# Four fused layers with windowed attention: the last half chunk of keys multiplied with V for both batches at once

## The chip, the cores and the metric

The kernel is one launch on one core of a Trainium2 chip. The metric is device time in microseconds (us), the median of several executions. A separate execution was recorded by the hardware profiler; its rows are called the trace here, and their sums the page. Engines are PE (TensorE matmuls; PEld is its loading of weights), DVE (VectorE), ACT (ScalarE), POOL (GpSimd) and SP (SyncE, which here only issues DMAs). L123 is line 123 of the kernel before.

## The reference

There are 64 batches of 64 tokens with 512 features, all in float32, and four layers, each added to its input:

```python
x = x + (einsum('bsi,bio->bso', x, W0[id]) + b0[id][:, None, :])     # a weight per batch
x = x + x @ W.T + delta                                              # LoRA: adapter per batch, rank 16
x = x + attention(x)                                                 # below
x = x + (einsum('bct,bcd->bdt', x, w3[subjects]) + bias[:, :, None]) # over the tokens of a batch
```

The attention has 8 query heads and 4 heads of keys and values, 64 wide. Queries and keys get an RMS norm and a rotary turn by their position `pos = kv_lens + t`. New keys and values are written into a cache of blocks; a query sees the positions from `pos - 255` to `pos`:

```python
allowed = (kpos <= pos) & (kpos > pos - WINDOW)       # WINDOW = 256
p = softmax(where(allowed, q @ k_all.T * SCALE, -inf))
o = (p @ v_all) @ Wo.T
```

So the 64 queries of a batch see a window of at most 319 positions, held as 320: two chunks of 128 and a half chunk of 64.

## The kernel before

The work goes by 32 tiles of 128 tokens, two batches each. Instructions run on each engine in the order in which the program issues them; that order is written out by hand, and the engines wait for each other by semaphores that follow from the tiles of memory they share. `bank()` hands out one bank of PSUM after the other from a ring of seven; an eighth (`pyp`) is for py.

**Phase 1 (lines 185 to 753, about 0 to 541 us).** For each tile: layer 0 with the two batches' gathered weights (`layer0`, L249: 128 rows by 64 columns, one batch in each half of the array; `add_bias`, L260, adds the bias to x on POOL), transposes (`turn0`, L273), layer 1 (L620 to L643), transposes back (L654), keys and values (L140, pk), and for older tiles the query product (pq), its norm and rotary turn (`turned`, L116 to L135) and transposes (`turn_q`, L170), whose result `qTs` goes by DMA to `qTd` in memory. Keys and values of each tile are stored to `kvd` (keep_kv). Old rows of the cache are fetched in the background by `copies` (a gather into `st` on POOL, L155, and a store to `kvd` on SP, L161 and L164): `other(i)` (L704) lets one or two of them go with each tile i > 5, and the last ones are stored when phase 1 ends. The biases come transposed through PE (`pb`) ahead of layer 0 of tile 0 (L668 to L673).

**Between the phases (L956 to L974).** SP issues the loads for phase 2: keys and values, queries, masks of tiles 0 and 1, `wo`, the query of tile 2. The queries of the last eight tiles (`LATE`) are made only here: product, `parts_q` on DVE and ACT, `turn_q`. Their `qTs` has two buffers in the pool `late`. `keys(0)` transposes the first tile's keys. The query of the last tile, 31, is made inside steps 0 to 3 of phase 2.

**Phase 2 (L975 to L1008, about 541 to 953 us).** Step s of the loop runs, in program order:

- `scores(s)`: eight products ps (L841), one bank each; DVE takes each with its mask and its maximum (L849, `pr` and `mx`), ACT the exponential (L853).
- `attend(s-1)`: the weights times V (L888), described below, and the copy of the sum `po` to `oT` (L906).
- `normalise(s)` on DVE (L861, L865): divides by the sums.
- on even s from 4 on `last(s-4)`: layer 3 of two tiles (pz, L928); then `project(s-2)`: times Wo (py, L916), added to x (L920).
- `keys(s+1)`: transposes of the next keys (pkt, L822, L828), copied by ACT (L823, L829).
- at s = 3 and 4 `turn_q` of a late query.
- `turn(s)`: transposes of the weights `pr` (ppt). For each of the four groups of heads g one bank with four blocks of 128 by 128 (L874: two full chunks of each of the two batches), copied to `pT[:, g]` by DVE and ACT in turn (L875). A fifth bank (L878) has the half chunks: `pr[:, g, 256:384]` is the half chunk of batch 0 next to that of batch 1, so that after the transpose partitions 0 to 63 hold batch 0's 64 positions and 64 to 127 batch 1's, each for the queries of both heads. ACT copies it whole to `pT[:, 4]` (L879).

`attend` sums in two banks, one per batch (`po[b2]`). 16 products have 128 positions each (tiles of 128 rows by 64 columns: two groups of heads share the array's columns). Eight more are for the half chunk, each with the 64 partitions of its batch (64 rows by 64 columns, a quadrant of the array). Each product is two instructions on PE.

Of the kernel before, what the change touches and what calls it, by code (L numbers as in the profile page):

```python
# [12 lines left out]
F32 = mybir.dt.float32  # L13
# [7 lines left out]
B, T, D = 64, 64, 512  # L21
NTOK = B * T
KC = D // 128
E = 16
NA, RANK = 8, 16
H, G, HD = 8, 4, 64
# [24 lines left out]
NT = NTOK // 128  # L51
# [8 lines left out]
def body(ctx: ExitStack, tc: tile.TileContext, a: dict, out: bass.AP):  # L60
    nc = tc.nc
    V, S, P, TE = nc.vector, nc.scalar, nc.gpsimd, nc.tensor
# [27 lines left out]
    late = ctx.enter_context(tc.tile_pool(name="late", bufs=1))  # L90
# [8 lines left out]
    def bank(name):  # L99
        return ring.tile([128, 512], F32, tag="ring", name=name)  # L100
# [65 lines left out]
    def run(parts):  # L166
        for _ in parts:
            pass

    def turn_q(i):  # L170
        qrf = qrs.pop(i)
        pqt = bank("pqt")
        for c in range(KC):
            TE.transpose(pqt[:, c * 128 : (c + 1) * 128], qrf[:, c * 128 : (c + 1) * 128], ident)  # L174
        qT = late.tile([128, 2, 2, 2, T], F32, name="qTs", bufs=2)
        for gp in range(2):
            S.copy(
                qT[:, gp].rearrange("p b h t -> p h b t"),
                pqt[:, gp * 256 : (gp + 1) * 256].rearrange("p (h b t) -> p h b t", h=2, b=2),
            )  # L180
        nc.sync.dma_start(
            qTd[i * 128 : (i + 1) * 128, :], qT.rearrange("p g b h t -> p (g b h t)")
        )

    with ExitStack() as pa:
# [57 lines left out]
        def layer0(i, bias=True):  # L243

            p0 = bank("p0")
            for c in range(KC):
                for h in range(2):
                    hs = slice(h * T, (h + 1) * T)
                    TE.matmul(p0[hs, :], xs[i][:, c, hs], w0s[i][h][:, c, :], start=c == 0, stop=c == KC - 1)  # L249
            w0s.pop(i)  # L250
            s0 = s0s[i] = wk.tile([128, D], F32, name="s0")
            S.copy(s0, p0)
            if bias:
                add_bias(i)

        def add_bias(i):

            x1 = x1s[i] = x1p.tile([128, KC, 128], F32, name="x1")
            for c in range(KC):
                P.tensor_tensor(  # L260
                    x1[:, c, :].rearrange("p (b t) -> p b t", t=T),
                    xs[i][:, c, :].rearrange("p (b t) -> p b t", t=T),
                    bc(biasT[:, c, 2 * i : 2 * i + 2, None], [128, 2, T]), ALU.add,
                )
            xs.pop(i)
# [54 lines left out]
        for h in range(2):  # L320
            hs = slice(h * B, (h + 1) * B)
# [11 lines left out]
        for h in range(2):  # L333
            hs = slice(h * 64, (h + 1) * 64)
# [331 lines left out]
        scalars()  # L666

        biasT = su.tile([128, KC, B], F32, name="biasT")  # L668
        pb = bank("pb")
        for c in range(KC):  # L670
            TE.transpose(pb[:, c * B : (c + 1) * B], brow[:, c * 128 : (c + 1) * 128], ident[:B, :B])
        S.copy(biasT.rearrange("p c b -> p (c b)"), pb[:, : KC * B])
        layer0(0)  # L673
        turn0(0)
        load_next(0)
        load_weight(wq, "wqT")
# [19 lines left out]
        def other(i):  # L696

            next(bg, None)
            next(bg, None)

            o = (i + 2) // 8
            if 0 < o < NT // 8 and i <= 8 * o + 2:
                next(turns.setdefault(o, rotation(o)), None)
            if i > 5:  # L704
                for _ in range(2 - i % 2):
                    next(old, None)

        for g in range(NG - 1):
# [5 lines left out]
            n, m = len(tiles[g]), len(tiles[g + 1])  # L714
# [63 lines left out]
    def load_q(i, queue=nc.sync):  # L778
        qT = qTs[i] = bp.tile([128, 2, 2, 2, T], F32, name="qT", bufs=4)
        queue.dma_start(  # L780
            qT.rearrange("p g b h t -> p (g b h t)"), qTd[i * 128 : (i + 1) * 128, :]
        )

    def load_mask(i):
        mb = mbs[i] = bp.tile([128, 2, NPOS], F32, name="mb", bufs=3)
        for h in range(2):
            r = nc.sync.value_load(cut[0:1, 2 * i + h : 2 * i + h + 1], min_val=0, max_val=WINDOW - 1)
            if h == 0:
                nc.sync.dma_start(mb[:, 0, :], maskd[:, bass.ds(r, NPOS)])
            else:  # L790
                nc.sync.dma_start(mb[:, 1, T:], maskd[:, bass.ds(r, WINDOW)])
                nc.sync.dma_start(mb[:, 1, :T], maskd[:, WINDOW:][:, bass.ds(r, T)])
# [23 lines left out]
    def keys(i):  # L816
        kv = kvs[i]
        kT = kTs[i] = bp.tile([128, 2, 2 * NPOS], F32, name="kT")
        for gp in range(2):
            pk = bank("pkt")  # L820
            for n, c in enumerate((0, 1, 4)):
                TE.transpose(pk[:, n * 128 : (n + 1) * 128], kv[:, c, gp * 128 : (gp + 1) * 128], ident)  # L822
            S.copy(kT[:, gp, :384], pk[:, :384])  # L823
        pk = bank("pkt")
        for gp in range(2):
            for c in range(2):
                n = 2 * gp + c
                TE.transpose(pk[:, n * 128 : (n + 1) * 128], kv[:, 2 + c, gp * 128 : (gp + 1) * 128], ident)  # L828
        S.copy(kT[:, :, 384:], pk.rearrange("p (g n) -> p g n", g=2))  # L829
# [37 lines left out]
    def turn(i):  # L867
        pr, _ = prs.pop(i)

        pT = pTs[i] = bp.tile([128, G + 1, 512], F32, name="pT")  # L870
        for g in range(G):
            pt = bank("ppt")
            for n, at in enumerate((0, 128, 384, 512)):
                TE.transpose(pt[:, n * 128 : (n + 1) * 128], pr[:, g, at : at + 128], ident)  # L874
            (S.copy if g % 2 else V.tensor_copy)(pT[:, g, :], pt)  # L875
        pt = bank("ppt")
        for g in range(G):
            TE.transpose(pt[:, g * 128 : (g + 1) * 128], pr[:, g, 256:384], ident)  # L878
        S.copy(pT[:, G, :], pt)  # L879

    def attend(i):
        kv, pT = kvs.pop(i), pTs.pop(i)
        oT = oTs[i] = bp.tile([128, KC, 2, T], F32, name="oT")
        po = [bank("po") for _ in range(2)]

        def product(b2, g, rows, n, c, m, start, stop):
            gp, g2 = divmod(g, 2)
            TE.matmul(  # L888
                po[b2][g2 * 64 : (g2 + 1) * 64, gp * 128 : (gp + 1) * 128],
                kv[rows, n, (G + g) * HD : (G + g + 1) * HD], pT[rows, c, m * 128 : (m + 1) * 128],  # L890
                start=start, stop=stop,
            )

        for b2 in range(2):
            for gp in range(2):
                for c in range(2):
                    for g in (2 * gp, 2 * gp + 1):
                        n = 2 * b2 + c

                        product(b2, g, slice(0, 128), n, g, n, gp == 0 and c == 0, False)  # L900
        for gp in range(2):
            for b2 in range(2):
                for g in (2 * gp, 2 * gp + 1):
                    product(b2, g, slice(b2 * 64, (b2 + 1) * 64), 4, G, g, False, gp == 1)
        for b2 in range(2):
            V.tensor_copy(oT[:, :, b2, :], po[b2][:, :256].rearrange("p (k t) -> p k t", t=T))  # L906

    def project(i, ring=False, parts=1):
        py, oT = bank("py") if ring else pyp.tile([128, 512], F32, name="py"), oTs.pop(i)
# [45 lines left out]

    for i in range(2):  # L956
        load_kv(i)
        load_q(i)
        load_mask(i)
    wo = bp.tile([128, KC, D], F32, name="wo", bufs=1)  # L960
    nc.sync.dma_start(wo, a["woT"].rearrange("(c p) f -> p c f", p=128))
    load_q(2)

    parts = {}
    for i in range(NT - LATE + 1, NT - 1):
        pq = product(i, wq, "pq")
        parts[i] = parts_q(i, pq, V, cs[i])
        next(parts[i])
        if i > NT - LATE + 2:
            turn_q(i - 2)  # L970
        if i - 1 in parts:
            run(parts.pop(i - 1))
        next(parts[i])
    keys(0)  # L974
    for s in range(NT):  # L975
        if s + 2 < NT:
            if s < 2:
                after_keys(s)
            load_kv(s + 2)
            load_mask(s + 2)  # L980
        if s and s + 2 < NT:
            load_q(s + 2)
        scores(s)
        if s >= 2:
            add_one(s - 2)
        if s:
            load_pair(s - 1)
            attend(s - 1)
        else:

            parts[NT - 1] = parts_q(NT - 1, product(NT - 1, wq, "pq", pyp), V, cs[NT - 1])
            turn_q(NT - 3)
        normalise(s, 0)
        if s == 1:
            next(parts[NT - 1])
            next(parts[NT - 1])
        normalise(s, 1)
        if s % 2 == 0 and s >= 4:
            last(s - 4)
        if s >= 2:  # L1000
            project(s - 2)
        if s + 1 < NT:
            keys(s + 1)
        if s in (3, 4):
            turn_q(NT - 5 + s)
        turn(s)
        if s in (2, 3):
            run(parts.pop(NT - 4 + s))  # L1008
    i = NT - 1
    load_pair(i)  # L1010
    add_one(i - 1)
# [60 lines left out]
```

## Time and profile before

| what | value |
|---|---|
| median of 11 runs | 955.61 us (951.97 to 960.15) |
| the profiled execution | 955.49 us |
| its span (first to last instruction) | 953.4 us |
| granted clock of PE, mean | 0.995 |
| busy: POOL | 404.5 us, 42% of the span |
| DMA | 260.97 MB, mean 274 GB/s |
| L841, ps, PE | 512 instructions, 81.9 us |
| L916, py, PE | 264 instructions, 118.3 us |
| L879, ACT's copy of the half chunks | 32 times, 592 ns each |
| L875, copies of 128x512 | DVE 64 times 691 ns; ACT 64 times 586 ns |
| L906, copies of po to oT, DVE | 64 times 419 ns |

How to read it: "busy" is the time in which an engine had an instruction; matmuls overlap in the array, so their mean time is longer than the distance between their starts. A group is named by line, engine, operation, the tiles it writes and reads, and its shapes; `64*64` behind a MATMUL is the part of the array that it uses (rows*columns), and the shape after it is the tile that is streamed. What stands last, with an arrow, is idle time of the engine before these instructions and what ended it. The chain of waits is followed back from the last instruction: each piece is the work that ended last before the next could start. The granted clock is the share of full speed at which PE was allowed to run.

### The profile page before, as it was taken

How to read it: one execution, taken by the hardware profiler on the slowest of the kernel's cores; microseconds unless marked ns; L12 is line 12 of the kernel's file. 1: busy time of each engine (PE TensorE's matmuls, PEld its weight loads, DVE VectorE, ACT ScalarE, POOL GpSimd, SP SyncE). 2: the span in 40 equal slices, each digit the busy share in tenths (PEclk: the TensorE clock that was granted, in tenths of full speed). 3: DMA queues.
4: the chain of work that ended last, by engine and by line, in shares of the span. 5: the costliest groups of instructions: out<-in, count | busy, mean ns of one | idle time of the engine just before them, and what ended most of it. 6: DMA issues, size and time to landing. Idle time of an engine off the chain costs nothing.

```text
span 953.4 us, 17790 instructions
## 1 busy us (share of the span) xinstructions
PE 922.0 (97%) x5397; PEld 508.8 (53%) x5397; DVE 613.3 (64%) x1736; ACT 415.4 (44%) x1084; POOL 404.5 (42%) x599
## 2 busy tenths in 40 slices
PE   4999999999999999999999799999999999999998
PEld 1344444444444444444344467666677777766665
DVE  4755998878573263532315778777777777777773
ACT  0312144221342231432213376666666666666663
POOL 3333466455354454444434554344444444444400
PEclk9999999999999999999999989999999999999999
DMA  7978999999999999999984774676666666666621
GB/s 250 352 279 275 336 374 316 387 400 328 378 348 380 393 327 392 394 337 395 385 296 178 264 257 141 212 222 194 206 201 206 202 206 203 205 209 206 205 64 46
DMA packets 133344, 260.97 MB, mean 274 GB/s; under 512 B 32737, under 2 KB 41570, under 8 KB 133250
## 3 DMA queue, kind: packets, MB, share of 16 engines
q1 hardware_dynamic: 108562, 178.61, 52.3%
q0 software_dynamic: 23280, 79.84, 25.4%
q10 hardware_dynamic: 1408, 1.39, 0.5%
q8 instruction: 43, 0.70, 0.3%
q14 instruction: 51, 0.42, 0.1%
HBM read 190.29 MB, written 69.50 MB: 272 GB/s over the span
## 4 chain that ended last, share of the span: by engine, by line
PE 70%; DMA 3%; DVE 2%; SPq 1%; ACT 1%; issue 0%; POOL 0%; ACTq 0%; DVEq 0%
PE py L916 12%; PE po L888 8%; PE ps L841 8%; PE p L635 7%; PE pk L140 7%; PE ppt L874 6%; PE p L249 6%; PE pq L140 5%; PE pkt L822 2%; PE ppt L878 2%; PE pkt L828 1%; PE pz L928 1%; DMA qTd<-qTs 1%; DMA w<-in_W 1%; PE px L654 1%; PE pqt L174 1%
## 5 line engine op out<-in xcount | busy, mean ns | idle before, releaser
L768 POOL DMA_INDIRECT kv<-kvd,idxn x128 | 126.4, 988 | 194.0 <-PE po L888 139.2
L853 ACT ACTIVATE pr<-pr,mx 128x320 f32<-128x320 f32 x256 | 140.1, 549 | 23.3 <-DVE mx L849 23.3
L849 DVE CUSTOM_DVE_ANT_0 pr<-ps,mb 128x320 f32<-128x320 f32 x256 | 107.9, 486 | 27.9 <-PE ps L841 27.5
L249 PE MATMUL p<-w,xt 128*64 128x512 f32 x512 | 121.1, 607 | 1.1 <-DMA w<-in_W 0.9
L916 PE MATMUL py<-wo,oT 128*128 128x512 f32 (+1 forms) x264 | 118.3, 591 | 0.0
L140 PE MATMUL pk<-wkv,x 128*128 128x512 f32 x256 | 115.4, 595 | 1.1 <-ACT x L656 1.1
L635 PE MATMUL p<-w,x 128*128 128x512 f32 x256 | 112.5, 596 | 0.0
L140 PE MATMUL pq<-wq,x 128*128 128x512 f32 x248 | 111.3, 593 | 0.0
L155 POOL DMA_INDIRECT st<-in_kvc,cidx x68 | 68.2, 1003 | 99.5 <-DMA kvd<-st 88.5
L274 DVE TENSOR_TENSOR x<-pt,x 128x512 f32<-128x512 f32 x32 | 22.0, 688 | 105.3 <-PE pt L273 98.2
L865 DVE TENSOR_SCALAR pr<-pr,sm 128x320 f32<-128x320 f32 x256 | 85.7, 396 | 2.2
L841 PE MATMUL ps<-kT,qT 64*128 64x320 f32 x512 | 81.9, 454 | 5.2 <-ACT kT L823 5.0
L888 PE MATMUL po<-pT,kv 128*64 128x128 f32 (+1 forms) x1536 | 82.1, 278 | 0.0
L888 PEld LDWEIGHTS po<-pT,kv 128*64 128x64 f32 (+1 forms) x1536 | 68.9, 135 | 19.8 <-DVE mx L849 13.6
L916 PEld LDWEIGHTS py<-wo,oT 128*128 128x128 f32 x264 | 47.5, 189 | 59.8 <-issue 58.6
L135 POOL TENSOR_TENSOR qr<-qn,sq 128x512 f32<-128x512 f32 x25 | 31.7, 1268 | 111.5 <-DVE qn L134 111.5
L635 PEld LDWEIGHTS p<-w,x 128*128 128x128 f32 x256 | 47.8, 190 | 58.2 <-issue 56.5
L249 PEld LDWEIGHTS p<-w,xt 128*64 128x64 f32 x512 | 35.6, 138 | 70.1 <-issue 66.4
L140 PEld LDWEIGHTS pk<-wkv,x 128*128 128x128 f32 x256 | 46.3, 190 | 49.4 <-issue 47.4
L140 PEld LDWEIGHTS pq<-wq,x 128*128 128x128 f32 x248 | 44.9, 190 | 46.2 <-issue 46.2
L875 DVE COPY pT<-ppt 128x512 f32<-128x512 f32 x64 | 44.1, 691 | 32.5 <-PE ppt L874 31.4
L874 PE MATMUL ppt<-ident,pr 128*128 128x128 f32 x512 | 62.5, 275 | 2.3 <-DVE pr L865 2.3
(191 smaller groups left out, 1309.7 us busy)
## 6 DMA issues: line engine op xcount, KB each, us to landing
w<-in_W SPq DMA_DIRECT2D x62, 1024.0 KB
kvd<-st SPq DMA_DIRECT2D x68, 512.0 KB
xt<-in_xT SPq DMA_DIRECT2D x32, 256.0 KB
x2d<-x2n SPq DMA_DIRECT2D x32, 256.0 KB
kvd<-kvn SPq DMA_DIRECT2D x32, 256.0 KB
qTd<-qTs SPq DMA_DIRECT2D x32, 256.0 KB
qT<-qTd SPq DMA_DIRECT2D x32, 256.0 KB
x2r<-x2d SPq DMA_DIRECT2D x32, 256.0 KB
```

Of the source, the lines that this page charges most:

```text
L140: TE.matmul(ps, x2s[i][:, c, :], w[:, c, :], start=c == 0, stop=c == KC - 1)
L155: P.indirect_dma_start(out=st, out_offset=None, in_=a["kvc"].rearrange("(n r) d -> n (r d)", r=2), in_offset=bass.IndirectOffsetOnAxis(ap= ...
L249: TE.matmul(p0[hs, :], xs[i][:, c, hs], w0s[i][h][:, c, :], start=c == 0, stop=c == KC - 1)
L635: TE.matmul(p1[i], x1s[i][:, c, :], w1[:, c, :], start=c == 0, stop=False)
L768: P.indirect_dma_start(out=kv[:, n, :], out_offset=None, in_=kvd, in_offset=bass.IndirectOffsetOnAxis(ap=at, axis=0),)
L841: TE.matmul(ps[g2][:, :NPOS], qT[rows, gp, b2].rearrange("p h t -> p (h t)"), kT[rows, gp, b2 * NPOS : (b2 + 1) * NPOS], start=True, stop= ...
L849: V.tensor_tensor_reduce(out=p, in0=ps[g2][:, :NPOS], in1=mb[:, b2, :], scale=-1.0, scalar=3.0e38, op0=ALU.add, op1=ALU.min, accum_out=mx[ ...
L853: S.activation(p, p, AF.Exp, bias=mx[:, g, b2 : b2 + 1], scale=-1.0, accum_out=sm[:, g, b2 : b2 + 1],)
L865: V.tensor_scalar(p, p, sm[:, g, b2 : b2 + 1], None, ALU.mult)
L874: TE.transpose(pt[:, n * 128 : (n + 1) * 128], pr[:, g, at : at + 128], ident)
L888: TE.matmul(po[b2][g2 * 64 : (g2 + 1) * 64, gp * 128 : (gp + 1) * 128], kv[rows, n, (G + g) * HD : (G + g + 1) * HD], pT[rows, c, m * 128 ...
L916: TE.matmul(py[:, fs], oT[:, c].rearrange("p b t -> p (b t)"), wo[:, c, fs], start=c == 0, stop=c == KC - 1,)
```

## The change

It does five things.

1. **The half chunk.** Two tiles `hT0` and `hT1` are filled with zeros once. `turn(s)` copies the fifth bank into `hT[s % 2]`, so that batch 0's half (partitions 0 to 63) goes to columns "batch 0" and batch 1's half (partitions 64 to 127) to columns "batch 1"; what lies beside stays zero. ACT copies the first half, DVE the second. `attend` then needs four products of 128 rows by 64 columns with 256 streamed columns in place of eight quadrants with 128, and sums both batches in one bank, which one copy takes to `oT`. `pT` is smaller by a fifth.
2. **Bias.** Layer 0 of tile 0 comes before the transposes of the biases, `add_bias(0)` behind them.
3. **Old rows** are fetched from tile 4 on rather than 6.
4. **Late queries.** Their `qTs` comes from the pool of phase 2 with four buffers.
5. **Order around the start of phase 2.** The loads of query 1, mask 1 and `wo` move behind the late queries, `wo` and query 2 behind step 0; the parts of query 31 move to other places in steps 1 to 3, and the two late `turn_q` from s = 3, 4 to s = 4, 5.

```diff
-    def turn_q(i):
+    def turn_q(i, pool=late):
...
-        qT = late.tile([128, 2, 2, 2, T], F32, name="qTs", bufs=2)
+        qT = pool.tile([128, 2, 2, 2, T], F32, name="qTs", bufs=2 if pool is late else 4)
...
+        layer0(0, False)
         pb = bank("pb")
...
-        layer0(0)
+        add_bias(0)
...
-            if i > 5:
+            if i > 3:
...
-        pT = pTs[i] = bp.tile([128, G + 1, 512], F32, name="pT")
+        pT = pTs[i] = bp.tile([128, G, 512], F32, name="pT")
...
-        S.copy(pT[:, G, :], pt)
+
+        ht = hTs[i % 2]
+        for b2, copy in enumerate((S.copy, V.tensor_copy)):
+            hs = slice(b2 * 64, (b2 + 1) * 64)
+            copy(ht[hs, :, b2, :], pt[hs].rearrange("p (g n) -> p g n", g=G))
...
+        po = bank("po").rearrange("p (k b n) -> p k b n", k=2, b=2)
         for b2 in range(2):
             for gp in range(2):
                 for c in range(2):
-                    for g in (2 * gp, 2 * gp + 1):
...
+                        TE.matmul(
+                            po[g2 * 64 : (g2 + 1) * 64, gp, b2], kv[:, n, (G + g) * HD : (G + g + 1) * HD],
+                            pT[:, g, n * 128 : (n + 1) * 128], start=b2 == 0 and gp == 0 and c == 0, stop=False,
+                        )
         for gp in range(2):
-            for b2 in range(2):
-                for g in (2 * gp, 2 * gp + 1):
-                    product(b2, g, slice(b2 * 64, (b2 + 1) * 64), 4, G, g, False, gp == 1)
-        for b2 in range(2):
-            V.tensor_copy(oT[:, :, b2, :], po[b2][:, :256].rearrange("p (k t) -> p k t", t=T))
+            for g2 in range(2):
+                g = 2 * gp + g2
+                TE.matmul(
+                    po[g2 * 64 : (g2 + 1) * 64, gp], kv[:, 4, (G + g) * HD : (G + g + 1) * HD],
+                    hTs[i % 2][:, g], start=False, stop=gp == 1,
+                )
+        V.tensor_copy(
+            oT.rearrange("p (k h) b t -> p k b h t", k=2), po.rearrange("p k b (h t) -> p k b h t", h=2)
+        )
...
     for i in range(2):
         load_kv(i)
-        load_q(i)
-        load_mask(i)
-    wo = bp.tile([128, KC, D], F32, name="wo", bufs=1)
-    nc.sync.dma_start(wo, a["woT"].rearrange("(c p) f -> p c f", p=128))
-    load_q(2)
+    load_q(0)
+    load_mask(0)
+
+    hTs = [bp.tile([128, G, 2, 128], F32, name=f"hT{n}", bufs=1) for n in range(2)]
+    for hT in hTs:
+        for b2 in range(2):
+            V.memset(hT[(1 - b2) * 64 : (2 - b2) * 64, :, b2, :], 0.0)
...
-            turn_q(i - 2)
+            turn_q(i - 2, bp)
...
     keys(0)
+    load_q(1)
+    load_mask(1)
+    wo = bp.tile([128, KC, D], F32, name="wo", bufs=1)
...
-            turn_q(NT - 3)
+            turn_q(NT - 3, bp)
+        if s == 2:
+            next(parts[NT - 1])
         normalise(s, 0)
-        if s == 1:
-            next(parts[NT - 1])
-            next(parts[NT - 1])
...
-        if s in (3, 4):
-            turn_q(NT - 5 + s)
+        if s in (4, 5):
+            turn_q(NT - 6 + s, bp)
+        elif s in (2, 3):
+
+            run(parts.pop(NT - 4 + s))
         turn(s)
-        if s in (2, 3):
-            run(parts.pop(NT - 4 + s))
+        if s == 0:
+            load_q(2)
+            nc.sync.dma_start(wo, a["woT"].rearrange("(c p) f -> p c f", p=128))
+        elif s == 1:
+            next(parts[NT - 1])
```

More of the change, by code (lines that the diff above doesn't have):

```diff
@@ L883, in attend @@
         oT = oTs[i] = bp.tile([128, KC, 2, T], F32, name="oT")
[L884 to L892, printed above, removed]
+        po = bank("po").rearrange("p (k b n) -> p k b n", k=2, b=2)
         for b2 in range(2):
@@ L896, in attend @@
                 for c in range(2):
-                    for g in (2 * gp, 2 * gp + 1):
-                        n = 2 * b2 + c
-                        product(b2, g, slice(0, 128), n, g, n, gp == 0 and c == 0, False)
-        for gp in range(2):
-            for b2 in range(2):
-                for g in (2 * gp, 2 * gp + 1):
-                    product(b2, g, slice(b2 * 64, (b2 + 1) * 64), 4, G, g, False, gp == 1)
-        for b2 in range(2):
-            V.tensor_copy(oT[:, :, b2, :], po[b2][:, :256].rearrange("p (k t) -> p k t", t=T))
+                    for g2 in range(2):
+                        g, n = 2 * gp + g2, 2 * b2 + c
+                        TE.matmul(
+                            po[g2 * 64 : (g2 + 1) * 64, gp, b2], kv[:, n, (G + g) * HD : (G + g + 1) * HD],
+                            pT[:, g, n * 128 : (n + 1) * 128], start=b2 == 0 and gp == 0 and c == 0, stop=False,
+                        )
+        for gp in range(2):
+            for g2 in range(2):
+                g = 2 * gp + g2
[6 more added lines that the diff above has]
+        )
     def project(i, ring=False, parts=1):
```

## The prediction

> **What bounds it.** First I read the page's line of busy times, then the busy time by stage, then the chain that ended last.
>
> ```profile
> PE 922.0 (97%) x5397; PEld 508.8 (53%) x5397; DVE 613.3 (64%) x1736; ACT 415.4 (44%) x1084; POOL 404.5 (42%) x599
> ```
> ```profile
> 541.00:546.00 5.00, 0.12 (x2) 0.12 (x2) 2.05 (x4) 2.53 (x8) 0.10 (x1) 0.83 0.27 104
> 546.00:551.00 5.00, 5.00 (x17) 2.88 (x18) 4.50 (x18) 4.58 (x12) 3.92 (x5) 0.50 0.71 211
> ...
> 558.00:571.00 13.00, 10.72 (x98) 8.02 (x98) 9.89 (x34) 10.00 (x27) 8.58 (x10) 0.89 0.95 312
> ...
> 700.00:800.00 100.00, 100.00 (x861) 69.05 (x854) 74.72 (x258) 66.50 (x190) 43.63 (x51) 1.00 0.63 200
> ```
>
> Columns: window, length, busy us and count of PE, PEld, DVE, ACT, POOL, then granted clock, DMA share, GB/s. From 600 to 900 us TensorE is busy all the time; DVE (74%), ACT (67%) and DMA (64%) have room. There each microsecond added to PE's own row of work, or to a wait of PE, is a microsecond of time, and nothing taken off another engine is. Only around 541–571, between the phases, does PE idle. The chain through one steady tile (start, length, link):
>
> ```profile
> 694.81 2.35 PE ps L841 x16
> 697.16 2.50 PE po L888 x48
> 699.66 0.86 PE pz L928 x8
> 700.52 3.63 PE py L916 x8
> 704.15 0.66 PE pkt L822 x6
> 704.80 0.44 PE pkt L828 x4
> 705.24 1.75 PE ppt L874 x16
> 706.99 0.44 PE ppt L878 x4
> ```
>
> It is PE alone: 12.63 us with pz, 11.77 without.
>
> **A. The half chunk on PE: +11.0 us.** Removed: per tile 16 instructions of 64*64; added: 8 of 128*64, each with 256 columns.
>
> ```profile
> L888 PE MATMUL po<-pT,kv 128*64 128x128 f32 x1024 | 63.0, 276 | 0.0
> L888 PE MATMUL po<-pT,kv 64*64 64x128 f32 x512 | 21.4, 282 | 0.0
> ```
>
> The means (276 and 282 ns) include pipelining, so I use the starts in the tile at 697 us. The 32 main instructions start in pairs, two 64-column halves of the array at once, 0.109 us apart. The 16 half instructions start **four at a time**: 698.990, 699.150, 699.259, 699.369. So today's half chunk is 4 steps of 0.109 = 0.436, plus 0.10 for the switch of tiling ahead of it (0.209 between starts instead of 0.109) and 0.05 on its first step. After the change 8 instructions go two at a time: 4 steps, but of 256 columns. PE's step is linear in columns (128: 0.109; 320: 0.269; 512: 0.429), so 256 is 0.216, and 4 steps are 0.863, with no switch in front. If py follows, the 0.10 switch behind it stays: 0.863 − 0.436 − 0.15 = +0.277. If pz follows (it starts 0.109 behind the half chunk today, since it is 64*64 too), the 0.15 of switching only moves in front of pz: +0.427. 17 attends of the first kind, 15 of the second: 17×0.277 + 15×0.427 = 4.7 + 6.4 = **+11.1, taken as +11.0**. The zeros are multiplied at full price: two batches in one pass saves instructions, but quadrants already ran both batches at once. Bounds: +8.9 (32 × 0.277, if pz pays no switch) to +13.7 (32 × 0.427); a gain is excluded as long as a step costs its columns.
>
> The Trainium skill, "TensorEngine Tiling (Array Packing)", Instruction Overhead, speaks for the change: each matmul carries about 60 cycles of overhead, so fewer, wider ones are better. By that estimate 8 fewer instructions at 25 ns give 0.2 us a tile, −6.4 us, and A would be +4.6. The row disagrees: 16 instructions in 0.49 us are 0.03 us each in all, and a step of 128 columns has only 2.5 ns beyond 256 cycles of 2.4 GHz.
>
> **B. The copy of the half chunk: +10.5 us.** Today ACT's L879 takes all 128 partitions in one copy, and DVE goes straight to the scores (L849):
>
> ```profile
> 682.98 2.42 PE L841 MATMUL ps<-kT,qT 64*128 64x320 f32 x16
> 683.14 0.59 ACT L879 COPY pT<-ppt 128x512 f32<-128x512 f32 x1
> ...
> 683.82 0.49 DVE L849 CUSTOM_DVE_ANT_0 pr<-ps,mb 128x320 f32<-128x320 f32 x1 [0.91 <-PE ps L841]
> ...
> 684.24 0.08 DVE L849 DVE_READ_ACCUMULATOR2_ANT mx<- 128x1 f32 x1
> ```
>
> Afterwards ACT copies partitions 0–63 (its 512 columns stay, so 0.59), and DVE partitions 64–127 (0.69 by L875's 128x512). Both write the same tile, and in the changed program DVE's copy waits for ACT's of the same step. ACT ends at 683.73, that is 0.75 after the first score; DVE's copy then runs from +0.80 to +1.49, the first L849 starts at +1.55 instead of +0.84, and signals at +2.05. Queued behind the waiting copy on DVE is every L849 of the tile. Who waits: the scores are 8 products through a ring of 7 banks, so the eighth needs the bank that the first L849 frees, and PE wants to start it at +1.72 (0.10 + 6 × 0.269). PE stands for 2.05 − 1.72 = 0.33–0.35; 31 tiles × 0.34 = **+10.5**. Bounds: 0 (a DVE copy that started with ACT's at 683.14 would end at 683.83, just when L849 starts today) to 31 × 0.5 = 15.5 (0.17 more for semaphores and a slower strided copy). I take the worked middle since all of its terms are rows. The rest of DVE's tile shifts by 0.7 and is covered: DVE idles 0.73 before oT (687.94), and the last normalise ends 0.86 us before ppt. oT's one copy (0.69 for 2 × 0.42 overlapping to 0.76) and the bank that po gives back lie beside PE: nothing.
>
> **C. Between the phases: −7.4 us.**
>
> ```profile
> 530.58 12.03 DMA qTd<-qTs
> ...
> 545.34 0.50 ACT kT L823
> 545.88 4.64 PE ps L841 x16
> 550.52 3.97 PE py L140 x8
> ```
>
> ACT's L177 waits for the third-last late query's buffer, its store sits in SP's queue behind qT, mask and wo, and lands at 542.6; keys(0) (L823) waits behind it on ACT. PE is idle 540.9–545.88, and the next 16 instructions run at clock 0.50: ps takes 4.64 instead of 2.35, py 3.97 instead of 3.44. Four buffers and the moved loads (qT(1), mask(1), wo, qT(2), with their DMAs) take this wait away. What is late next: DVE, in order, now has four memsets of hT before the first late query; they wait for phase 1's last kvd store (landed 523.09; about 522.1 when the st stores on SP, L164, are 20 us earlier). No row has this memset; four at the 0.06 us of a 128x1 one (L405) would be 0.2, four at the 0.69 of L875's copy of 512 columns 2.8; I take 2.0, nearer to the copy, since 512 columns have to be written. The late queries then come 1.45 later through DVE: transposes end about 542.35, kT(0) 542.9, first score **543.4** (545.88), pq of 31 at 546.2 (550.52, with the clock kept), ppt 551.2 (556.02). At s=1 DVE's ss, rs, qn of query 31 stood between the normalise steps (565.36–567.25); they move, and ps(2) comes at 563.85 instead of 570.68, warm (−0.5): **−7.4**. Behind that, sq/qn/qr now run ahead of the pT copies at s=2 and 3 and turn_q moves to s=4, 5; today such DVE work costs 0.9 us twice (ps 3.3 instead of 2.4 at s=3, 4), and I add **+1.4** for what is worse. Bounds of C: 0 (memsets and a late store eat it, clock 0.50 again) to −13.9 (all idle and cold time from 516 to 596: 0.25 + 4.98 + 0.23 + 2.05 + 1.8 + 4.6).
>
> The row shows half clock already after the 2.05 us idle at 565.85–567.90 (ppt steps 0.213 for 0.109). The Trainium skill, "TensorE: Matmul & The Clock Gate", puts the limit at idle gaps of about 3 us; by that my 1 us gap is free, by the row it may not be, and then C loses some 2 us.
>
> **D. Phase 1: −0.5 us.** Layer 0 of tile 0 no longer waits for the bias, but its last weights land only at 14.86 and ACT copies s before biasT; the bias adds on POOL (4 × 0.42) follow, and layer 0's sum may be 0.4 later; PE waits at 26.9 for W0 of tile 1 in any case. Three old-row gathers (POOL) and their stores (SP) move from 515 to about 65 us, beside DMA at 0.9–1.0; PE idles only 3.8 us from 100 to 500. Between −3 and +0.5.
>
> **Sum**: 11.0 + 10.5 − 7.4 + 1.4 − 0.5 = +15.0. The profiled run is 955.49 (span 953.4, 2.09 around it; the median of 11 is 955.61): **970.5**.
>
> **Rivals.**
> - *The copy is hidden* (B = 0): if DVE's copy is not held, or the eighth bank is free. For it: ACT and DVE read one bank side by side, po gives a bank back. Against: the wait in the program, ring of 7. 955.49 + 4.5 = 960.0; with D at −3, 957.5.
> - *Faster*: the transition returns all idle and cold time, 13.9, B = 0, and D brings 0.5 to 3: 955.49 + 11.0 − 13.9 − 1.7 = 950.9. It decides when C exceeds A + B. For it: the 541–571 rows; against: DVE's memsets, and A in each of 32 tiles.
> - *The change does not do what it says between the phases*: the last kvd store lands at 523.1, memsets take 2.3 and PE goes cold again: C = 0. 955.49 + 11.0 + 10.5 + 1.4 − 0.5 = 977.9.
>
> **Chances.** Forecast 0.50 (966–975), hidden copy 0.30 (957–964; a third of it within no change), no gain between the phases 0.12 (976–980), faster 0.08. A measurement tells about 0.3% (2.9 us) from no change: faster 0.08, same 0.10, slower 0.82. The range 957 to 979 leaves out the faster case and the outer edges, under 0.2.
>
> **What would show it.** A: po L888 in the chain at 2.77 rather than 2.50, its 256-column group with 256 instructions; pz later by 0.15. B: DVE's hT copy starting at ACT's end, ps at 2.69 instead of 2.35 with PE waiting for mx L849; PE's busy share below 100 in 600–900. C: ps(0) near 543.4 with clock near 1.0. Wrong if PE's step of 256 columns is shorter than 0.216, if ps stays at 2.35, or if PE waits near 543–565 for a new releaser.

## The result and the profile after

The changed kernel takes **979.73 us** (median of 8 runs, 977.58 to 982.48) against 955.62 us (31 runs, 951.97 to 960.15): ratio 1.0249, 95% interval 1.0232 to 1.0266. It is slower by 24.1 us; 970.5 was forecast, and 979.73 lies 0.7 above the range. The profiled execution has a span of 978.6 us, 25.2 more.

The page's busy times of the changed kernel:

```profile
PE 949.4 (97%) x5141; PEld 519.3 (53%) x5141; DVE 635.5 (65%) x1740; ACT 416.1 (43%) x1084; POOL 404.6 (41%) x599
```

PE has 256 instructions fewer and is busy 27 us longer. The chain through a steady tile (start, length, link) shows where in phase 2:

```profile
704.27 2.79 PE ps L842 x16
707.05 1.90 PE po L897 x32
708.95 0.86 PE po L904 x8
709.81 1.02 PE pz L932 x8
710.83 3.63 PE py L920 x8
```

po is 1.90 + 0.86 = 2.76 (2.50 before), pz 1.02 (0.86), ps 2.79 (2.35). From the first score of one tile to that of the next, a tile with pz takes 13.47 us instead of 12.61, one without 12.45 instead of 11.75. The groups of lines (busy, mean ns | idle before and its releaser) and the timeline give the reason for ps (L842, L850 and L884 of the changed kernel are the scores, the maxima and the copies to hT):

```profile
L904 PE MATMUL po<-hT,kv 128*64 128x256 f32 x256 | 33.1, 379 | 0.0
...
L884 DVE COPY hT<-ppt 64x512 f32<-64x512 f32 x32 | 22.2, 695 | 25.1 <-ACT hT L884 25.0
```
```profile
704.20 2.85 PE L842 MATMUL ps<-kT,qT 64*128 64x320 f32 x16
704.36 0.58 ACT L884 COPY hT<-ppt 64x512 f32<-64x512 f32 x1
704.97 0.69 DVE L884 COPY hT<-ppt 64x512 f32<-64x512 f32 x1 [0.84 <-ACT hT L884]
705.70 0.49 DVE L850 CUSTOM_DVE_ANT_0 pr<-ps,mb 128x320 f32<-128x320 f32 x1
```

DVE idles 25 us in all for ACT's half of the copy, and its first L850 starts 1.50 us after the first score (0.84 before). Counted from the first score, the eighth starts at 2.053 instead of 1.725, as its bank comes free. It is the wait that costs, not the copy itself, by an estimate from these rows: a copy of 0.69 that started with ACT's at 704.36 would end at 705.05, and 705.04 is 0.84 after the first score, where the first maximum started before.

The table of windows hides this stall: it has PE at 100.00 of 100 from 600 to 900 us here too.

```profile
700.00:800.00 100.00, 100.00 (x771) 69.07 (x771) 74.66 (x240) 62.90 (x177) 39.80 (x46) 1.00 0.61 194
```

The seventh score, whose end is modelled, counts as running while the eighth waits. The chain and the distance between tiles show it, the busy share does not.

Two more places differ. In phase 1, the start of layer 0 of tile 11 is 6.0 us later than before (161.75 against 155.73), that of tile 31 4.5, and the last four products of keys and values start at 507.68 instead of 502.52. The timeline of POOL, DVE and PE in the changed kernel, 100 to 161 us:

```profile
106.43 0.96 POOL L155 DMA_INDIRECT st<-in_kvc,cidx  x1 [8.89 <-DMA kvd<-st]
...
108.04 0.76 DVE L133 TENSOR_TENSOR sq<-qn,sg 128x256 f32<-128x256 f32 x2 [2.67 <-POOL sg L110]
...
152.42 0.66 PE L273 MATMUL pt<-ident,s 128*128 128x128 f32 x4 [1.35 <-ACT s L252]
154.62 6.76 PE L140 MATMUL pk<-wkv,x 128*128 128x512 f32 x8 [1.54 <-ACT x L656]
```

Read it downwards: a gather on POOL waits 8.9 us for a store to free its buffer, the products sg (of the gains and the sine) queue behind it, DVE waits 2.7 us for them. DVE is busy 83% of 100 to 200 us and hasn't caught up at tile 10: ACT's copies, which stand behind DVE's sums, are late, PE idles 1.35 and 1.54 us, and then the windows (length, PE, PEld, DVE, ACT, POOL, granted clock) show the clock down, so that pk takes 6.76 instead of 3.70. The windows of the changed kernel, and pk of the same tile in the kernel before:

```profile
140.00:150.00 10.00, 10.00 (x38) 4.21 (x37) 9.11 (x16) 0.68 (x3) 5.48 (x10) 1.00 0.94 324
150.00:160.00 10.00, 7.10 (x14) 2.89 (x13) 8.55 (x13) 5.85 (x11) 8.05 (x12) 0.70 0.84 261
```
```profile
151.66 3.70 PE L140 MATMUL pk<-wkv,x 128*128 128x512 f32 x8 [0.54 <-ACT x L656]
```

Between the phases, DVE and PE of the changed kernel:

```profile
528.32 2.37 DVE L968 MEMSET hT<- 64x512 f32 x4 [3.11 <-DMA kvd<-kvn]
...
535.46 0.63 PE L174 MATMUL pqt<-ident,qr 128*128 128x128 f32 x4 [3.04 <-DVE rs L126]
535.92 5.29 PE L140 MATMUL pq<-wq,x 128*128 128x512 f32 x8
...
551.71 3.01 PE L842 MATMUL ps<-kT,qT 64*128 64x320 f32 x16 [1.17 <-issue]
...
580.07 3.70 PE L920 MATMUL py<-wo,oT 128*128 128x512 f32 x8 [1.63 <-DVE qn L128]
```

The memsets stand 3.1 us for the last kvd store and take 2.4; PE then waits 3.04 us for the first late query (0.25 in the kernel before) and runs its next product at half clock (5.29 for 3.60). In return the wait of 4.98 us ahead of the first scores is 1.17.

### The profile page after: what moved, and what is told of

Same layout as the page of the kernel before. It is cut to its first block, busy times and chain, and to the rows that moved or that the text cites. A ratio compares the mean times of both kernels' runs of the same rounds, so it can differ in the third digit from the quotient of the medians.

```text
span 978.6 us, 17278 instructions
## 1 busy us (share of the span) xinstructions
PE 949.4 (97%) x5141; PEld 519.3 (53%) x5141; DVE 635.5 (65%) x1740; ACT 416.1 (43%) x1084; POOL 404.6 (41%) x599
## 4 chain that ended last, share of the span: by engine, by line
PE 91%; DVE 3%; DMA 2%; ACT 1%; issue 1%; SPq 1%; ACTq 0%; POOL 0%; DVEq 0%
PE py L920 12%; PE p L635 12%; PE p L249 11%; PE pk L140 11%; PE pq L140 9%; PE ps L842 9%; PE po L897 6%; PE ppt L875 6%; PE po L904 3%; PE pkt L823 2%; DMA w<-in_W 2%; PE pz L932 2%; PE pkt L829 1%; PE ppt L879 1%; PE px L654 1%; PE pqt L174 1%
## 5 line engine op out<-in xcount | busy, mean ns | idle before, releaser
L140 PE MATMUL pk<-wkv,x 128*128 128x512 f32 x256 | 118.4, 608 | 2.1 <-ACT x L656 2.1
L850 DVE CUSTOM_DVE_ANT_0 pr<-ps,mb 128x320 f32<-128x320 f32 x256 | 107.8, 486 | 1.0
L842 PE MATMUL ps<-kT,qT 64*128 64x320 f32 x512 | 92.1, 449 | 1.5 <-issue 1.2
L133 DVE TENSOR_TENSOR sq<-qn,sg 128x256 f32<-128x256 f32 (+1 forms) x128 | 40.1, 354 | 47.3 <-POOL sg L110 45.4
L842 PEld LDWEIGHTS ps<-kT,qT 64*128 64x128 f32 x512 | 55.5, 186 | 27.3 <-issue 6.6
L123 ACT ACTIVATE ss<-ss,epst 128x4 f32<-128x4 f32 (+1 forms) x64 | 19.1, 299 | 113.6 <-DVE ss L122 113.5
L824 ACT COPY kT<-pkt 128x384 f32<-128x384 f32 x64 | 27.6, 483 | 85.0 <-PE pkt L823 85.0
```

Source lines behind the costliest of these rows:

```text
L140: TE.matmul(ps, x2s[i][:, c, :], w[:, c, :], start=c == 0, stop=c == KC - 1)
L842: TE.matmul(ps[g2][:, :NPOS], qT[rows, gp, b2].rearrange("p h t -> p (h t)"), kT[rows, gp, b2 * NPOS : (b2 + 1) * NPOS], start=True, stop= ...
L850: V.tensor_tensor_reduce(out=p, in0=ps[g2][:, :NPOS], in1=mb[:, b2, :], scale=-1.0, scalar=3.0e38, op0=ALU.add, op1=ALU.min, accum_out=mx[ ...
```

## The experiments

Lines are those of the changed kernel; times are medians, ratios are to the kernel before, run beside each. "Less" is against the changed kernel's 979.73 us. The theory of all of them is the same: the change has four prices, for PE's columns (A), the split copy (B), the memsets and their wait (between the phases, C) and the early old rows (phase 1, D), and a gain from the moved loads; each price falls away with its own edit.

**e1, both copies on ACT**

```diff
-        for b2, copy in enumerate((S.copy, V.tensor_copy)):
+        for b2, copy in enumerate((S.copy, S.copy)):
```

> The changed kernel (979.73 us), but ACT copies both halves of the half chunk, so that DVE has no copy that waits for ACT's. Theory (the wait delays the first L850 on DVE, and with it the bank that the eighth score needs): ps in the chain goes from 2.79 back to 2.35, 31 tiles by 0.44 = 13.6 us less, about 966 us; ACT's extra 0.59 us a tile lies in its idle time before the first exponential. Rival (the scores are late because po now takes one bank of the ring in place of two, so that the ring's order shifted): ps stays at 2.79, about 980 us.

Measured: 967.54 us (ratio 1.0119, interval 1.0092 to 1.0146), 12.2 less. The chain of e1:

```profile
710.92 2.35 PE ps L842 x16
713.27 1.90 PE po L897 x32
715.17 0.86 PE po L904 x8
716.03 3.63 PE py L920 x8
```

ps is 2.35 again with po still in one bank: the ring is not the cause, DVE's copy with its wait is. In this trace tiles take 12.02 and 13.04 us, 0.43 less each; what is left above the kernel before, 0.27 and 0.43, is A. Between the phases PE waits here too, yet its next product runs at full clock:

```profile
534.90 0.63 PE L174 MATMUL pqt<-ident,qr 128*128 128x128 f32 x4 [3.20 <-DVE rs L126]
535.36 3.60 PE L140 MATMUL pq<-wq,x 128*128 128x512 f32 x8
```

**e2, old rows from tile 6 on**

```diff
-            if i > 3:
+            if i > 5:
```

> The changed kernel, but old rows are fetched from tile 6 on again. Theory (the early gathers fill the five st buffers, a gather on POOL then waits 8.9 us for a store, cos and sin gains behind it make DVE late, and PE idles twice at 151 to 155 us and runs at half clock to 161): layer 0 of tile 31 starts about 4.5 us earlier (470.3), the time falls by 5.2 to about 974.5 us. Rival (the half clock at 155 us came by chance in the profiled execution, or from the bias order at the start): within 1 us of 979.7.

Measured: 976.96 us (1.0208, 1.0176 to 1.024), 2.8 less, where 5.2 were expected. The start of layer 0 of tile 31 is at 469.79, 5.0 earlier, so phase 1's loss is gone entirely; but the memsets now stand for a store of a query, the next wait of PE for the late query is 3.34 us, and its clock stays down longer:

```profile
523.66 2.38 DVE L968 MEMSET hT<- 64x512 f32 x4 [3.41 <-DMA qTd<-qTs]
...
530.81 1.09 PE L174 MATMUL pqt<-ident,qr 128*128 128x128 f32 x4 [3.34 <-DVE rs L126]
531.69 6.01 PE L140 MATMUL pq<-wq,x 128*128 128x512 f32 x8
```

The theory holds for the place; of 5.0 us only 2.8 reach the end.

**e3, quadrants from hT, the zeros not read**

```diff
-                TE.matmul(
-                    po[g2 * 64 : (g2 + 1) * 64, gp], kv[:, 4, (G + g) * HD : (G + g + 1) * HD],
-                    hTs[i % 2][:, g], start=False, stop=gp == 1,
-                )
...
+                    hs = slice(b2 * 64, (b2 + 1) * 64)
+                    product(b2, g, hs, 4, hTs[i % 2][hs, g, b2], False, gp == 1)
```

(the products as in the kernel before, po in two banks, two copies to oT)

> The changed kernel with its copies to hT, its memsets and its order, but the half chunk is multiplied in quadrants of 64*64 from hT, each batch in its own bank, as before; the zeros aren't read. Theory (columns cost their time, and the four quadrants ran side by side): po goes from 2.76 to 2.50 and pz from 1.02 to 0.86, 17 by 0.27 and 15 by 0.43 = 11.0 us less, about 968.7 us. Rival (the time sits in the waits around it, and PE's own price is mostly hidden by DVE's lateness): 3 us less or nothing, 977 to 980 us.

Measured: 969.1 us (1.014, 1.0112 to 1.0168), 10.6 less. Its chain:

```profile
711.69 2.79 PE ps L842 x16
714.48 2.50 PE po L893 x48
716.97 3.63 PE py L922 x8
```

po is 2.50, ps stays at 2.79: A and B are separate, and each is on the path in full.

**e4, memsets on POOL**

```diff
-            V.memset(hT[(1 - b2) * 64 : (2 - b2) * 64, :, b2, :], 0.0)
+            P.memset(hT[(1 - b2) * 64 : (2 - b2) * 64, :, b2, :], 0.0)
```

> The changed kernel with the four memsets of hT on POOL in place of DVE. Theory (DVE's memsets wait for phase 1's last kvd store and hold the late queries' norms behind them): PE's 3.04 us ahead of pqt at 535 us and the 1.7 us of half clock behind it go, about 4.7 us less, 975 us. Rival (the first late query waits for the same store or for DVE's keys work anyway, or the idle time moves to the first scores, whose kT copy comes late): within 1.5 us of 979.7.

Measured: 975.18 us (1.0197, 1.0168 to 1.0226), 4.55 less. PE's timeline in e4:

```profile
531.88 0.63 PE L174 MATMUL pqt<-ident,qr 128*128 128x128 f32 x4 [0.18 <-DVE rs L126]
532.34 3.60 PE L140 MATMUL pq<-wq,x 128*128 128x512 f32 x8
```

Wait and half clock are gone together, as the theory has it.

**e5, the half chunk undone** (`turn` and `attend` of the kernel before, no hT; the rest of the change stays)

```diff
-        ht = hTs[i % 2]
...
+        S.copy(pT[:, G, :], pt)
```

> The changed kernel with the half chunk as it was (quadrants from pT, one copy by ACT, no hT and no memsets); bias order, early old rows, four buffers and moved loads stay. Theory (terms add): 979.7 less 11.0 for PE's half chunk, 12.2 to 13.6 for the copy and 4.6 for the memsets: 950.5 to 952, that is 4 to 5 us below the kernel before, with phase 1 still some 5 us longer in the trace. Rival (the moved loads save nothing without the longer steps that cover their landing): 956 or more.

Measured: 950.26 us (0.9947, 0.9923 to 0.9971), 0.2 under what the sum of the terms gave. Phase 1 is not 5 us longer, as expected, but 2.1 (layer 0 of tile 31 at 472.38, 470.29 in the kernel before): PE waits nearly as long as in the changed kernel, and pk stays at full clock.

```profile
151.98 0.66 PE L273 MATMUL pt<-ident,s 128*128 128x128 f32 x4 [1.20 <-ACT s L252]
154.18 3.70 PE L140 MATMUL pk<-wkv,x 128*128 128x512 f32 x8 [1.54 <-ACT x L656]
```

**e6, e5 with old rows from tile 6 on** (the edits of e5 and e2)

> The same with old rows from tile 6 on again: what is left of the change is the bias order, the four buffers and the moved loads and parts. Theory: 2.8 to 5 us below the run with early old rows, about 947 us; against the kernel before that is the gain between the phases alone, 8.4 us, worked out from the run with the memsets on POOL (first score of tile 7 comes 3.8 us earlier counted from the last keys product, with 4.6 us of the dearer half chunk in it). Rival (early rows pay at the end of phase 1 what they cost at its start): same as with early rows, 951.

Measured: **948.83 us** (0.9928, 0.9905 to 0.995), faster than both kernels. It is 1.4 us below e5, where 2.8 to 5 were expected: the early rows cost here too, less than the 2.8 of e2, and medians of six runs don't tell 1.4 well. Its PE between the phases:

```profile
543.50 3.28 PE L842 MATMUL ps<-kT,qT 64*128 64x320 f32 x16 [1.16 <-issue]
546.71 3.70 PE L140 MATMUL py<-wq,x 128*128 128x512 f32 x8
...
570.93 3.70 PE L917 MATMUL py<-wo,oT 128*128 128x512 f32 x8 [1.68 <-DVE qn L128]
```

**e7, the half chunk alone** (the kernel before with hT, memsets, `turn` and `attend` of the changed one)

```diff
-        S.copy(pT[:, G, :], pt)
+        ht = hTs[i % 2]
+        for b2, copy in enumerate((S.copy, V.tensor_copy)):
...
```

> The kernel before with the half chunk alone changed (zeros, hT, memsets on DVE ahead of the late queries). Theory: 955.6 + 11.0 + 13.6 = 980.2 us, and 0 to 4 more for the memsets, since PE waits for the query's store until 545 us in any case: 980 to 984. Rival (the half chunk needs the moved loads to pay, and its cost is smaller where PE waits elsewhere): under 976.

Measured: 984.95 us (1.0298, 1.0265 to 1.0331), a little above what the theory gave. PE waits 4.41 us for the first late query, and at s = 3 and 4 twice 1.9 us for L849 (of the kernel before), where the norms of late queries on DVE follow the late copy and stand ahead of the eight maxima:

```profile
590.09 0.80 PE L841 MATMUL ps<-kT,qT 64*128 64x320 f32 x2 [1.88 <-DVE mx L849]
590.82 3.07 PE L896 MATMUL po<-pT,kv 128*64 128x128 f32 x32
```

The rival, that the half chunk costs less without the moved loads, falls.

**e8, six st buffers**

```diff
-        op = pa.enter_context(tc.tile_pool(name="op", bufs=5))
+        op = pa.enter_context(tc.tile_pool(name="op", bufs=6))
```

> The changed kernel with six st buffers for old rows in place of five; nothing else moves. Theory (the sixth gather waits for the first store to land, and POOL's gains and then DVE stand behind it): the 8.9 us wait of POOL before 106 us is gone, DVE's sq no longer waits 2.7 us for sg, layer 0 of tile 31 starts 2 to 4.5 us earlier, the time falls by 2 to 3 us to about 977. Rival (it is the DMA traffic of the early rows that delays phase 1, whatever the buffers): no change, 979.7.

Measured: 975.12 us (1.0192, 1.0157 to 1.0226), 4.6 less, more than the 2 to 3 expected. POOL's waits from 60 to 130 us (in total, times, longest) in e8; in the changed kernel the same row reads 14.5, 3, 8.9:

```profile
POOL st L155 <- DMA kvd<-st: 7.1, 2, 3.6
```

DVE's longest wait for sg is 0.6 (2.67), and layer 0 of tile 11 to 31 starts as early as without the early rows (tile 31: 469.94). The early traffic itself costs nothing that the trace shows; the full ring of buffers does.

**e9, e12, e13, the half chunk without waits** (the edits of e1, e2 and e4 together)

> The changed kernel with its half chunk and zeros, but with every wait around it taken away: both copies to hT on ACT, memsets on POOL, old rows from tile 6 on. Theory (what is left of the half chunk is PE's price alone): 948.8 us of the version without the half chunk, plus 11.0 for the columns = 959.8, still above the kernel before (956). Rival (the half chunk is only as dear as its waits): 950, below it.

> The same kernel as in the run before it (half chunk with zeros, both copies to hT on ACT, memsets on POOL, old rows from tile 6 on), since there the kernel before itself took 974.5 us, with idle time of ACT in each second tile that no other trace has, so that the terms can't be added up on it. Theory, where the kernel before takes about 956: PE's price of the columns alone is left, 948.8 + 11.0 = 959.8 us, ratio 1.004, tiles of 12.02 and 13.04 us. Rival (the 1.0176 of that run was the price): about 972 us.

> The half chunk with zeros and no waits around it, together with the changed kernel and the version without the half chunk, so that the three stand beside each other whatever time the kernel before takes here. Theory: 11.0 us above the version without the half chunk and 13.6 + 2.8 + 4.6 = 21 us below the changed kernel; where the kernel before takes 956, that is 959.8. Rival (both copies on ACT cost as much as the wait on DVE did): less than 12 us below the changed kernel.

Measured: 992.96, 994.8 and 995.65 us (1.0176, 1.0202, 1.0189), well above the ratio of 1.004 that the theory gave. Beside these runs, and beside e10, e11, e14 and e15, the kernel before itself takes 974.5 to 978.0 us, so they can't be set against e1 to e8. In their traces, in every second tile, DVE and ACT start their copies of pT 2 to 3 us late, and PE stands for them; in e11, which differs from the kernel before at the start alone:

```profile
757.08 1.29 DVE L876 COPY pT<-ppt 128x512 f32<-128x512 f32 x2 [3.45 <-PE ps L842]
757.19 1.07 ACT L876 COPY pT<-ppt 128x512 f32<-128x512 f32 x2 [2.24 <-PE ps L842]
757.82 1.94 PE L842 MATMUL ps<-kT,qT 64*128 64x320 f32 x12 [0.91 <-DVE pT L876]
```

What holds them isn't shown: the PE work that they need was done at about 754.7. The expectations speak of a first chip, but the chip's number on record doesn't tell the two apart: it is 10 for e5 to e8, beside which the kernel before takes 956.31, and 10 again for e13 to e15, beside which it takes 977.97.

**e14, e15, the changed kernel and e6 beside e13**

> The changed kernel as it is, beside the other two. Theory: ratio 1.025 to the kernel before, as on the first chip, if what that chip showed holds here. Rival (where the kernel before takes 974.5, its engines start late in each second tile, and this hides part of the change's cost): a ratio under 1.022.

> The version without the half chunk and with old rows from tile 6 on, beside the other two. Theory: ratio 0.993 to the kernel before, as it was measured; the best of the kernels here. Rival: within 0.3% of the kernel before, if its gain between the phases belongs to the first chip.

Measured: 1017.33 (1.0406, 1.0383 to 1.043) and 975.43 us (0.9963, 0.9941 to 0.9985). Neither the theory of e14 (1.025) nor its rival (under 1.022) holds, and e15 lies between its theory (0.993) and its rival (0.997 to 1.003). The waits cost 1017.33 − 995.65 = 21.7 us, as expected (21); what is left of the half chunk costs 995.65 − 975.43 = 20.2, not 11.0. The chain of e13 goes over ACT's late copies to pT and hT, while e1's chain from 610 to 900 us has PE's work alone:

```profile
709.42 0.59 ACT pT L876
710.01 0.48 ACT hT L884
710.51 0.59 ACT hT L884
711.14 0.81 PE ps L842 x4
```

So here the copies on ACT are no longer free, and even a tile without pz takes 12.47 in e13 where e1 had 12.02; how the 20.2 divide into columns and copies isn't shown. The price of the columns alone is measured by e3, and by the tiles of e1. The ratios differ from those of the earlier runs, their order doesn't.

**e10, an earlier part of query 31** (e6 with the part moved)

```diff
-        if s == 2:
-            next(parts[NT - 1])
...
-        elif s == 1:
+        if s < 2:
             next(parts[NT - 1])
```

> The version without the half chunk and with old rows from tile 6 on (948.83 us), in which the first two parts of query 31 run behind turn(0) and turn(1), not behind turn(1) and ahead of step 2's normalise. Theory (py of step 2 waits 1.68 us for qn of query 31, which reads the bank that py needs): that wait goes and nothing waits in its place, since DVE and ACT stand idle between steps 0 and 1: about 947.2 us. Rival (the same DVE work delays the first L850 of step 1 or 2 as much, or ACT's square root ahead of an exponential costs PE a wait): within 0.7 us of 948.8 or more.

Measured: 969.23 us (0.9932, 0.9911 to 0.9953), beside 974.49 of the kernel before; e15, the version without it, had 0.9963 (0.9941 to 0.9985). PE's wait for qn ahead of py is gone in its trace, but the intervals overlap: not decided.

**e11, the bias order alone**

```diff
+        layer0(0, False)
         pb = bank("pb")
...
-        layer0(0)
+        add_bias(0)
```

> The kernel before with the order of layer 0 of tile 0 and the biases alone changed. Theory (W0 of tile 0 and of tile 1 set the start in either order): layer 0 of tile 2 starts within 0.5 us of 41.15, time 955.6 to 956.6. Rival (the bias order carries part of the loss of phase 1, by the half clock that the trace of the changed kernel shows at 20 to 30 us): 957 to 958.5.

Measured: 975.11 us (median of 10, one of them 4533.29) beside 974.49 (0.9993, 0.9978 to 1.0008), layer 0 of tile 2 within the forecast bound, that of tile 3 at 46.08 (46.15 before). It is worth nothing, though the granted clock at 20 to 30 us fell to 0.83 in the changed kernel.

## Why the prediction was right or wrong

The sign, the likeliest mechanism and the size of A were right; the sum was 9 us short, some 2 to 3 of it by B, 4 by C and 3 to 5 by D. By number the result fell into the case that had a chance of 0.12. Set side by side (us; measured by the difference of medians):

| step | forecast | measured |
|---|---|---|
| A, PE's columns | +11.0 | +10.6 (e3) |
| B, split copy | +10.5 | +12.2 (e1); 13.6 by 31 × 0.44 in the trace |
| C with the +1.4 behind it | −6.0 | −2.2 (e6 against before −6.8, memsets +4.55 by e4) |
| D, phase 1 | −0.5 | +2.8 (e2), +4.6 (e8), +1.4 without hT (e5 less e6) |
| sum | +15.0 | +23.4 with e2; the result is +24.1 |

The kernel before took 955.62 us beside the changed kernel, 956.09 beside e1 to e4 and 956.31 beside e5 to e8, so 0.5 to 0.7 of a difference can come from the group of runs and not from the edit. Beside its own 956.31, e6 is −7.5, C −2.9 and the sum 22.7.

- **A** was right to a hundredth in the chain (0.86 for four steps of 256 columns, pz + 0.16). The Trainium skill, "TensorEngine Tiling (Array Packing)", Instruction Overhead, gives each matmul an overhead of about 60 cycles; the prediction's estimate from that figure would have made A 4.6. e3 measures 10.6.
- **B**: mechanism, place and waiting instruction were right, and the eighth score started 0.33 us late as worked out. The step that was mis-sized: *"PE stands for 2.05 − 1.72 = 0.33–0.35"* left out that the seventh and eighth score no longer run side by side and the eighth's second instruction comes 0.373 behind its first instead of 0.269. That is the 0.10 up to 0.44.
- **C**: the gain of the moved loads was sized well (−6.8 without memsets). What failed is *"I take 2.0 … The late queries then come 1.45 later"*. The memsets took 2.4 and their store landed at 527.97, 5.9 us after where I put it, most of that by D (in e2, without D, they start at 523.66). PE's wait was 3.04, where about 1 was forecast, and the half clock behind it cost a further 1.7 in this execution. The prediction had named the clock as a risk of some 2 us and left it out of its sum. That half clock is not certain: after 3.20 in e1 there was none. The rival without gain between the phases named memsets and a cold PE; its 977.9 was the nearest figure, but in part by luck, since it kept C at 0, B at 10.5 and D at −0.5.
- **D** failed in sign. *"Three old-row gathers (POOL) and their stores (SP) move … beside DMA at 0.9–1.0"* counted bandwidth and PE's slack, and not the five buffers behind which POOL has to stand, nor that DVE at 83 to 87% in 100 to 200 us has no room to make up 2.7 us. e8 shows it: a sixth buffer, and the loss is gone. Of the 4.5 us in the trace of the changed kernel 3.1 are the half clock of pk (6.76 for 3.70), which e5 doesn't have after nearly the same waits; that the measured prices of D run from 1.4 to 4.6 may come from this, but isn't shown.
- The sign to look for in the busy share (*"PE's busy share below 100 in 600–900"*) was wrong, see above.

The rivals of a hidden copy and of a faster kernel fall: ps is 2.79, and C is a few us, not 13.9.

What stays open: why the copies start late where e9 to e15 ran, and A's price there. Open is also whether DVE's copy stands for ACT's because both write one tile or because both read one bank of PSUM: no run here separates the two.

## What to carry to other kernels

Where four quadrants of the array already ran side by side, merging their work into wider products beside zeros was paid by the column; count steps times columns, not instructions. A copy split over two engines, from one bank into one tile, was here a wait of the second on the first, and cost what was queued behind it: 12 us, against nothing for both halves on ACT in e1. A background fetch that is moved earlier can fill its ring of buffers, and the engine that issues it then stands with its other work behind it; here one more buffer was enough.

## What the hardware showed beyond that

PE's clock fell after less idle time than one gap of 3 us: single gaps of 2.05 us (565.85 in the kernel before) and 1.88 us (ahead of 590.09 in e7, where po then takes 3.07 for 1.97) were enough, and so were 1.35 and 1.54 us within 4 us of each other (granted clock 0.70 at 150 to 160 us), while 1.63 us alone (580.07) left py at 3.70. But the length alone doesn't decide: 3.20 us in e1 left pq at 3.60, and 1.20 and 1.54 us in e5 left pk at 3.70. What a gap of this size costs differs from one trace to the next, so a single trace doesn't price it; what decides isn't shown.

The Trainium skill, "TensorE: Matmul & The Clock Gate", Why this matters for your kernels, asks for no idle gaps over about 3 us; these rows have shorter gaps that cost the clock and one of 3.20 that did not.

And the same kernel took 955.6 to 956.3 us beside some runs and 974.5 to 978.0 beside others, with ratios of 1.025 and 1.041 for the same change.
